# Two residual 5x5 convolution layers on one core: layer 1's v inside x's buffer, layer 2's row combinations by ScalarE and adding transfers, column filtering in more chunks of layer 2

## The chip, the cores and the metric

The kernel runs on one core of one Trainium2 chip. The metric is the device time of one execution in microseconds (us), median of the runs. A time taken from the profile belongs to one profiled execution.

## The reference

The input x is 8 images of 32 channels of 252 x 252 float32. Two layers of the same form follow each other:

```python
# _gn: normalisation over 16 groups of 2 channels; conv: 5x5, reflected borders, 32 -> 32 channels
x = x + _L0_conv_ref(_gn(x), L0_conv_weight)
x = x + _L1_conv_ref(_gn(x), L1_conv_weight)
```

The convolution's centre lies one pixel off (the reference shifts its weight by `-k // 2`, which is -3), so layer 1's result is kept with its own border columns and rows before layer 2 reads it.

## The kernel before, in words

**Layout.** An image is split by the parity of its columns and rows. The four parities of the 32 channels fill the 128 partitions, so the 5x5 filter becomes a 3x3 filter over 128 channels. The rows of an image are worked in 8 chunks of 16 rows of partitions (`ROWS`), in 4 groups of 4 (`NT`). In the code l is 0 for layer 1 and 1 for layer 2, b the image and c the chunk.

**Rows: a transform with six points.** Along the rows each group of four outputs is computed by six products at points 0 to 5 in place of twelve. `transform` makes the inputs of these points from the rows of a chunk (VectorE): v, differences of rows two apart (`row_pairs`), and u, two combinations "row + four times (or minus four times) another row" (`row_quads` L576 and L577, `last_rows` L584). From u come points 2 and 1 (`point2` L592, `point1` L602), from v points 4, 3, 0 and 5 (`point4` L596, `point3` L599, `points05` L609). For layer 2 v isn't made by VectorE: `row_sums` copies rows by a transfer that GpSimd issues (L557) and adds the others by two adding transfers (L559, L560). The copy waits until L609 of the chunk before has read the one buffer of v, the adding transfers wait for the copy.

**Columns: all or filtered.** `conv` multiplies on TensorE: three products for each of points 2, 4 (`m`, in PSUM), 1, 3 (`pairs`) and then 0, 5 (`sums`). In chunks for which `by_columns` says so, points 0 and 5 are column-filtered: `columns` (L612 on) makes sums and differences of neighbouring columns on VectorE, eight products of half width (L707) take the place of six of full width, and `column_parts` (L787 on) puts the halves together. ScalarE and VectorE move results out of PSUM (`seed`, `evacuate`, `difference`, `inner`, `outer`, `outer_columns`).

**Layer 1's result.** `keep` writes sums for layer 2's normalisation and the border columns of y (`reflect`: four narrow copies on ScalarE, L869 to L872). Layer 2's result is interleaved into o by ScalarE (L925) and stored.

**Loading x.** `load` (SP's queue) brings a chunk of x into one of two buffers xs; each row has 256 elements. For most chunks only the partitions of one column parity are loaded (`once`): they hold the odd columns, `even_columns` (ScalarE, L159) copies one into the other half of the partitions. GpSimd fills `borders` (L148 to L154). Layer 1's `transform` reads the even columns only.

**Order.** There is no scheduler: each step is entered in a table with a time in us, and the steps are issued in order of these times; at run time each engine follows its order and waits for semaphores.

```python
order = [(0, 0, c) for c in range(NCH)]
for k in range((B - 1) * NCH):
    order += [(1 + k // NCH, 0, k % NCH), (k // NCH, 1, k % NCH)]
```

So layer 1's chunk of one image alternates with layer 2's chunk of the image before. I call two such chunks a pair. `begin(i)` is the time at which slot i (the i-th chunk of `order`) starts on TensorE: 13.6 us from one slot to the next where both chunks are filtered. A chunk's transform runs in the slot before its own, its outputs of points 0 and 5 leave PSUM up to two slots later. For layer 2 `two` is the start of the slot two before its own, in which L557 (at `two` + 1.45) and L559 and L560 (at `two` + 8.4) stand.

Names that the steps touch: `row_sums`, `row_quads`, `last_rows`, `row_pairs`, `points05` and `columns` in `transform`; `column_parts` in `conv`; `reflect` in `keep`; `load`, `borders`, `even_columns`; `by_columns`. The pool `vpool` has one buffer for each tag; layer 1's v has the tag "v", layer 2's "va" (the last chunks use both), u has "u12".

Of the kernel before, what the change touches and what calls it, by code (L numbers as in the profile page):

```python
# [42 lines left out]
F32 = mybir.dt.float32  # L43
# [6 lines left out]
P = 128  # L50
# [6 lines left out]
def tile_conv_preact_x2(ctx: ExitStack, tc: tile.TileContext, x: bass.AP, w0: bass.AP, w1: bass.AP, out: bass.AP):  # L57
# [34 lines left out]
    def at(t: float, fn, *args, **kw):  # L92
        table.append((t, len(table), fn, args, kw))
# [67 lines left out]
    def once(b: int, c: int) -> bool:  # L161

        return c != NCH - 1 and (c != 1 if b > 1 else c != 3 if b else True)

    def copied_late(b: int, c: int) -> bool:

        return once(b, c) and (b > 1 or (b == 1 and c > 3))

    def parts(b: int, c: int):

        if once(b, c):
            return ((0, 10), (10, 6)) if (b, c) == (0, 0) else ((0, 2), (2, 14))
        return ((0, ROWS),) + (((ROWS, 2),) if c == NCH - 1 else ())
# [363 lines left out]
    def transform(t0: float, t1: float, b: int, l: int, c: int, free: float = -100.0, now=(0, 0, 0)):  # L537

        wi = WIN[l]
        got = {}  # L540
        sent = l == 1 and (b, c) != (0, 0)

        def source():
            if l == 0:
                nxt = xs[b, c + 1] if c + 1 < NCH else xtail[b]
                return xs[b, c][:, :, 0:256:2], nxt[:, :, 0:256:2]
            return ytile[b, c], ytile[b, c + 1] if c + 1 < NCH else ytail[b]

        def row_sums(add: bool):

            t, nxt = source()
            if not add:

                i = max(order.index((b, l, c)) - order.index((B - 2, 1, NCH - 2)), 0)
                got["v"] = vpool.tile([P, ROWS, wi], F32, tag=("va", "v")[i % 2], name=f"v_{b}_{l}_{c}")
                got["vt"] = got["v"].rearrange("p (t i) w -> p t i w", i=4)
                G.dma_start(got["v"], t)  # L557
            else:
                G.dma_start(got["v"][:, 0 : ROWS - 2], t[:, 2:ROWS], accum_op=ALU.add)  # L559
                G.dma_start(got["v"][:, ROWS - 2 : ROWS], nxt[:, 0:2], accum_op=ALU.add)  # L560

        def row_pairs(j0: int = 0, j1: int = NT):
            if j0 == 0:
                got["v"] = vpool.tile([P, ROWS, wi], F32, tag="v", name=f"v_{b}_{l}_{c}")
            v, (t, nxt) = got["v"], source()
            r0, r1 = 4 * j0, min(4 * j1, ROWS - 2)
            (V.tensor_add if l else V.tensor_sub)(v[:, r0:r1], t[:, r0 + 2 : r1 + 2], t[:, r0:r1])  # L567
            got["vt"] = v.rearrange("p (t i) w -> p t i w", i=4)

        def row_quads(j0: int = 0, j1: int = NT):  # L570
            if j0 == 0:
                got["u"] = vpool.tile([P, 2, NT, wi], F32, tag="u12", name=f"u12_{b}_{l}_{c}")
            u1, u2, (t, nxt) = got["u"][:, 0], got["u"][:, 1], source()
            r0, k1 = 4 * j0, min(j1, NT - 1)
            f = 4.0 if l else -4.0
            stt(u1[:, j0:j1], t[:, r0 + 1 : 4 * j1 : 4], f, t[:, r0 + 3 : 4 * j1 : 4], ALU.mult, ALU.add)  # L576
            stt(u2[:, j0:k1], t[:, r0 + 2 : 4 * k1 : 4], f, t[:, r0 + 4 : 4 * k1 + 1 : 4], ALU.mult, ALU.add)  # L577

        def last_rows():

            u2, (t, nxt) = got["u"][:, 1], source()
            if not sent:
                (V.tensor_add if l else V.tensor_sub)(got["v"][:, ROWS - 2 : ROWS], nxt[:, 0:2], t[:, ROWS - 2 : ROWS])
            stt(u2[:, NT - 1], t[:, ROWS - 2], 4.0 if l else -4.0, nxt[:, 0], ALU.mult, ALU.add)  # L584

        def point2(j0: int = 0, j1: int = NT):
            if j0 == 0:
                t = tpool.tile([P, 2, NT, wi], F32, tag="t24", bufs=1, name=f"t24_{b}_{l}_{c}")
                if not fixed:
                    fixed.append(vpool.tile([P, 2, NT, WMAX], F32, tag="t13", name="t13"))  # L590
                ts[b, l, c] = {0: t, 1: fixed[0][:, :, :, 0:wi]}
            V.tensor_sub(ts[b, l, c][0][:, 0, j0:j1], got["u"][:, 1, j0:j1], got["u"][:, 0, j0:j1])  # L592

        def point4(j0: int = 0, j1: int = NT):
            vt = got["vt"][:, j0:j1]
            stt(ts[b, l, c][0][:, 1, j0:j1], vt[:, :, 1], -2.0, vt[:, :, 2], ALU.mult, ALU.add)  # L596

        def point3():
            stt(ts[b, l, c][1][:, 1], got["vt"][:, :, 1], 2.0, got["vt"][:, :, 2], ALU.mult, ALU.add)  # L599

        def point1():
            stt(ts[b, l, c][1][:, 0], got["u"][:, 1], norm[b, l][1][:, 1:2], got["u"][:, 0], ALU.add, ALU.add)  # L602

        def points05():
            if by_columns(b, l, c):
                t = vpool.tile([P, NT, 2, wi], F32, tag="u12", name=f"t05_{b}_{l}_{c}")
            else:
                t = tpool.tile([P, NT, 2, wi], F32, tag="t05", name=f"t05_{b}_{l}_{c}")
            stt(t, got["vt"][:, :, 0:2], 4.0 if l else -4.0, got["vt"][:, :, 2:4], ALU.mult, ALU.add)  # L609
            ts[b, l, c][2] = t  # L610

        def columns():  # L612

            t, (m, mo) = ts[b, l, c][2], evens_odds(l)
            sd = vpool.tile([P, 2, NT, 2, m], F32, tag="sdiff", name=f"sdiff_{b}_{l}_{c}")
            d = tpool.tile([P, NT, 2, 2, m], F32, tag="t05", name=f"d05_{b}_{l}_{c}")
            odd, even = t[:, :, :, 1 : 2 * m : 2], t[:, :, :, 2 : 2 * m + 1 : 2]
            V.tensor_add(sd[:, 0], odd, even)
            V.tensor_sub(sd[:, 1], even, odd)
            if m == mo:  # L620
                f = "p t e (m a) -> p (t e) a m"
                V.tensor_sub(
                    d.rearrange("p t e a m -> p (t e) a m"),
                    t[:, :, :, 0 : 2 * m].rearrange(f, a=2), t[:, :, :, 2 : 2 * m + 2].rearrange(f, a=2),
                )
            else:
                V.tensor_sub(d[:, :, :, 0], t[:, :, :, 0 : 2 * m : 2], t[:, :, :, 2 : 2 * m + 1 : 2])
                V.tensor_sub(d[:, :, :, 1, 0:mo], odd[:, :, :, 0:mo], t[:, :, :, 3 : 2 * mo + 2 : 2])
            ts[b, l, c][2] = d, sd

        if (b, l, c) == order[0]:
            at(t0 - 33.3, row_quads, 0, 2)
            at(t0 - 31, point2, 0, 2)
            for fn in (row_pairs, point4):
                at(t0, fn, 0, 2)
            at(t0 + 0.2, row_quads, 2, 4)
            at(t0 + 0.2, row_pairs, 2, 4)
            at(t0 + 0.2, last_rows)
            at(t0 + 0.2, point2, 2, 4)
            at(t0 + 0.2, point4, 2, 4)  # L640
            at(t0 + 4.9, point1)
            at(t0 + 5.5, point3)
            at(t0 + 6.2, points05)
        else:
            if sent:
                two = begin(order.index((b, l, c)) - 2)
                at(two + 1.45, row_sums, False)
                at(two + 8.4, row_sums, True)
            else:
                at(t0, row_pairs)  # L650
            for dt, fn in ((2, row_quads), (3.2, last_rows), (3.6, point2)):
                at(t0 + dt, fn)
            at(max(t0 + 4.2, free + 9.45) if sent else t0 + 4.2, point4)
            at(max(t0 + 5.5, free + 7.8), point1)
            at(max(t0 + 5.6, free + (11.1 if by_columns(*now) else 10.25)), point3)
            at(t1, points05)
            if by_columns(b, l, c):
                at(t1 + 1.5, columns)
# [184 lines left out]
    def keep(t1: float, t2, b: int, c: int, got):  # L843
# [17 lines left out]

        def reflect():
            lo, hi = (1 if c == 0 else 0), (ROWS - 1 if c == NCH - 1 else ROWS)
            y, copy, r = got["y"], A.copy, slice(lo, hi)

            def negated(dst, src):
                A.activation(dst, src, AF.Copy, scale=-1.0)
# [101 lines left out]
    def by_columns(b: int, l: int, c: int) -> bool:  # L969
        if l == 0:  # L970
            return c < NCH - 1 and (b > 1 or (b == 1 and c > 1))
        return c in {B - 1: (1, 2, 3, 4, 5), B - 2: (1, 2, 3)}.get(b, (1, 2, 3, 5, 7))

    own = [5.1 if i in at_once else 1.7 if by_columns(*n) else 0.0 for i, n in enumerate(order)]
    late = [0.0 if i in at_once else 1.7 if by_columns(*n) else 5.1 for i, n in enumerate(order)]
# [60 lines left out]
    for i, (b, l, c) in enumerate(order):  # L1036
# [11 lines left out]
        if i + 1 < len(order):  # L1048
# [3 lines left out]
            if nl == 0 and 2 < k < len(inputs):  # L1052
                kb, kc = inputs[k]
                for part in parts(kb, kc):
                    if copied_late(kb, kc):
                        at(t0 + 9.5, load, kb, kc, *part)
                        at(begin(i + 2) + 4.0 if part[0] else t1 + 5.5, borders, kb, kc, *part)
                        at(begin(i + 3) + 4.0 if part[0] else t1 + 9.35, even_columns, kb, kc, *part)
                        continue
# [77 lines left out]
```

## Time and profile before

| | |
|---|---|
| Time, median of 3 runs (lowest, highest) | 1879.63 us (1878.62, 1879.75) |
| Profiled execution: its own time | 1879.27 us |
| Its span, first to last instruction | 1877.5 us |
| Mean granted TensorE clock | 0.994 |
| q1, transfers issued by SP: MB, share of the DMA engines' span | 230.73, 49.8% |
| q0, transfers issued by GpSimd: MB, share | 134.20, 29.3% |

Read a row of groups as: line, engine, operation, output<-input by the program's names, shape, count, then busy us and mean ns of one. A row of the timeline begins with start and duration in us. A row of windows gives for a stretch the busy us (and instructions) of PE, PEld, DVE, ACT and POOL, then the granted clock, the mean DMA share and GB/s. PE is TensorE, DVE VectorE, ACT ScalarE, POOL GpSimd. A row of waits says which engine and line waited for which: total us, times, longest.

### The profile page before, as it was taken

How to read it: one execution, taken by the hardware profiler on the slowest of the kernel's cores; microseconds unless marked ns; L12 is line 12 of the kernel's file. 1: busy time of each engine (PE TensorE's matmuls, PEld its weight loads, DVE VectorE, ACT ScalarE, POOL GpSimd, SP SyncE). 2: the span in 40 equal slices, each digit the busy share in tenths (PEclk: the TensorE clock that was granted, in tenths of full speed). 3: DMA queues.
4: the chain of work that ended last, by engine and by line, in shares of the span. 5: the costliest groups of instructions: out<-in, count | busy, mean ns of one | idle time of the engine just before them, and what ended most of it. 6: DMA issues, size and time to landing. Idle time of an engine off the chain costs nothing.

```text
span 1877.5 us, 20381 instructions
## 1 busy us (share of the span) xinstructions
PE 1839.2 (98%) x5194; PEld 966.0 (51%) x5194; DVE 1731.2 (92%) x3030; ACT 1493.8 (80%) x2781; POOL 396.2 (21%) x855
## 2 busy tenths in 40 slices
PE   5999999999999999999999999999999999999998
PEld 4444455545555555555555455554555555555455
DVE  7988799999999999999999899999999999997796
ACT  5886788878887888888898798987898876765575
POOL 4543111131112211122111311113111141110211
PEclk8999999999999999999999999999999999999999
DMA  9877578878888877987878967888878866775785
GB/s 275 203 179 180 151 209 199 210 194 202 217 202 219 194 209 192 221 223 173 220 193 206 235 175 205 205 204 204 212 202 198 214 165 140 179 174 148 195 212 125
DMA packets 207110, 369.07 MB, mean 197 GB/s; under 512 B 19088, under 2 KB 173968, under 8 KB 196752
## 3 DMA queue, kind: packets, MB, share of 16 engines
q1 hardware_dynamic: 178832, 230.73, 49.8%
q0 software_dynamic: 27600, 134.20, 29.3%
q10 hardware_dynamic: 560, 2.83, 0.4%
q8 instruction: 41, 0.67, 0.2%
q14 instruction: 77, 0.63, 0.1%
HBM read 167.15 MB, written 67.39 MB: 125 GB/s over the span
## 4 chain that ended last, share of the span: by engine, by line
PE 80%; DVE 7%; DMA 6%; ACT 3%; issue 3%; SPq 0%; POOL 0%; DVEq 0%; ACTq 0%; POOLq 0%
PE m L685 28%; PE pairs L685 28%; PE sums L707 7%; PE extra L707 6%; PE sums L685 6%; PE extra L685 4%; DMA v<-y 2%; DMA st<-in_x_dram 1%; DMA v<-ytail 1%; DMA xs<-in_x_dram 1%; ACT o L925 1%; DVE sd L748 1%; DVE t L609 1%; DMA wraw<-in_L_conv_weight_dram 1%; DMA out_dram<-o 0%
## 5 line engine op out<-in xcount | busy, mean ns | idle before, releaser
L685 PE MATMUL pairs<-t,u 128*128 128x504 f32 (+2 forms) x1548 | 692.9, 586 | 5.4 <-ACT pairs L729 3.3
L685 PE MATMUL m<-t,u 128*128 128x508 f32 (+3 forms) x1560 | 674.8, 581 | 3.4 <-DVE u L526 1.9
L685 PEld LDWEIGHTS m<-t,u 128*128 128x128 f32 x1560 | 294.2, 189 | 317.1 <-issue 297.0
L685 PEld LDWEIGHTS pairs<-t,u 128*128 128x128 f32 x1548 | 290.2, 189 | 320.1 <-issue 289.1
L925 ACT COPY o<-y 64x508 f32<-64x508 f32 x496 | 327.5, 660 | 8.6
L748 DVE SCALAR_TENSOR_TENSOR sd<-sd,pairs 128x504 f32<-128x504 f32 (+2 forms) x258 | 164.2, 671 | 19.5 <-PE pairs L685 15.2
L707 PEld LDWEIGHTS extra<-sdiff,wc 128*128 128x128 f32 x680 | 125.9, 189 | 98.1 <-issue 47.8
L707 PE MATMUL extra<-sdiff,wc 128*128 128x252 f32 (+3 forms) x680 | 173.0, 376 | 3.4 <-ACT extra L711 2.3
L860 ACT ACTIVATE junk<-y,negk 128x1008 bf16<-128x1008 f32 (+1 forms) x144 | 147.4, 1024 | 31.1 <-PE extra L707 14.5
L557 POOL DMA_DIRECT2D v<-y x63 | 35.7, 567 | 622.7 <-DVE t L609 608.4
L737 ACT COPY sd<-m 128x504 f32<-128x504 f32 (+2 forms) x258 | 136.9, 581 | 33.3 <-DVE sums L794 28.1
L609 DVE SCALAR_TENSOR_TENSOR t<-v 128x1024 f32<-128x1024 f32 (+1 forms) x128 | 157.7, 1232 | 5.4 <-PE sums L685 5.4
L707 PE MATMUL sums<-d,u 128*128 128x252 f32 (+3 forms) x680 | 157.4, 374 | 0.0
L707 PEld LDWEIGHTS sums<-d,u 128*128 128x128 f32 x680 | 127.6, 189 | 24.9 <-issue 9.0
L685 PE MATMUL sums<-t,u 128*128 128x508 f32 (+5 forms) x312 | 133.6, 577 | 0.0
L567 DVE TENSOR_TENSOR v<-xs 128x1792 f32<-128x1792 f32 (+1 forms) x65 | 130.2, 2003 | 1.2
L241 ACT ACTIVATE st<-st,negk 128x1134 f32<-128x1134 f32 x98 | 121.7, 1242 | 3.2
L559 POOL DMA_DIRECT2D v<-y x63 | 54.3, 862 | 329.1 <-DMA v<-y 329.1
L159 ACT COPY xs<-xs 64x1792 f32<-64x1792 f32 (+2 forms) x97 | 109.3, 1129 | 13.4 <-POOL xs L151 11.1
L729 ACT ACTIVATE pairs<-m,means 128x504 f32<-128x504 f32 (+1 forms) x129 | 84.2, 653 | 44.5 <-PE m L685 36.0
L785 ACT ACTIVATE y<-sums 128x504 f32<-128x504 f32 (+1 forms) x158 | 94.5, 634 | 28.3 <-PE sums L707 19.2
L235 ACT ACTIVATE st<-st 128x1134 f32<-128x1134 f32 x98 | 112.5, 1148 | 5.0 <-DMA st<-in_x_dram 3.2
(174 smaller groups left out, 2529.7 us busy)
## 6 DMA issues: line engine op xcount, KB each, us to landing
v<-y POOLq DMA_DIRECT2D x63, 1032.0 KB, 6.1
st<-in_x_dram SPq DMA_DIRECT2D x111, 567.0 KB, 6.1
out_dram<-o SPq DMA_DIRECT2D x480, 126.0 KB, 5.9
v<-y POOLq DMA_DIRECT2D x63, 903.0 KB, 7.7
xs<-in_x_dram SPq DMA_DIRECT2D x96, 441.0 KB, 8.4
xs<-in_x_dram SPq DMA_DIRECT2D x44, 504.0 KB, 12.0
u<-ud SPq DMA_DIRECT2D x15, 1152.0 KB, 6.0
xs<-in_x_dram SPq DMA_DIRECT2D x16, 472.5 KB, 9.3
```

The source lines that it names most:

```text
L159: copy(t[64:128, :, 0:256:2], t[0:64, :, 1:256:2])
L235: A.activation(junk, src, AF.Identity, accum_out=acc[:, 0, i : i + 1])
L241: A.activation(junk, src, AF.Square, bias=negk, accum_out=acc[:, 1, i : i + 1])
L567: (V.tensor_add if l else V.tensor_sub)(v[:, r0:r1], t[:, r0 + 2 : r1 + 2], t[:, r0:r1])
L609: stt(t, got["vt"][:, :, 0:2], 4.0 if l else -4.0, got["vt"][:, :, 2:4], ALU.mult, ALU.add)
L685: T.matmul(dst, u[:, k, 2 - i, :], rhs[:, j0 + i0 : j0 + i1, i : i + wo], start=(i == 0 and not add), stop=(i == 2), skip_group_check=add,)
L707: T.matmul(dst[:, 0, use], w, rhs[:, use], start=(i == 2), stop=True, skip_group_check=(i != 2))
L737: A.copy(got["sd"][:, 1 + e], m24[e][:, 0:n])
L748: stt(d, d, -2.0, pairs13[e][:, 0:n], ALU.mult, ALU.add)
L785: A.activation(y, src, AF.Copy, scale=1.0 - 2 * i, **total(3 * i))
L860: A.activation(dst, src, AF.Square, bias=negk, scale=1.0 if i else -1.0, accum_out=acc[:, 1, at_ : at_ + 1])
L925: copy(got["o", h][halves[s], 0:m, cp::2], got["y"][halves[cp], r : r + m, :])
```

## The change

1. Layer 1's v (from image 1, chunk 4 on) is written by VectorE into the odd columns of x's own buffer, which nothing reads after `even_columns`; it needs no buffer of its own. x's buffer is then released only after `points05`. So the loads two chunks later (`deferred`) are entered later, in two parts for all chunks.
2. For 50 chunks of layer 2 u isn't made by VectorE. ScalarE writes four times the rows into a buffer with the freed tag "v" (`four_times`), and GpSimd issues three adding transfers that add the other rows (`outer_rows`), ahead of the copy that begins v.
3. `by_columns` covers chunks 1 to 7 of layer 2 (before: 1, 2, 3, 5, 7), and 1 to 4 of the last image but one (before: 1 to 3).
4. The four copies of border columns in `reflect` are issued on GpSimd in chunks 1 to 6.

```diff
+    def among_columns(b: int, c: int) -> bool:
+        return b > 1 or (b == 1 and c > 3)
+    def deferred(b: int, c: int) -> bool:
+        i = inputs.index((b, c))
+        return i > 1 and among_columns(*inputs[i - 2])
     def parts(b: int, c: int):
+        if deferred(b, c):
+            return ((0, 2), (2, 14)) + (((ROWS, 2),) if c == NCH - 1 else ())
...
+        sent_u = l == 1 and (b, c) > (0, 4) and order[order.index((b, l, c)) - 1][1] == 0
...
+        def four_times():
+            got["u"] = vpool.tile([P, 2, NT, wi], F32, tag="v", name=f"ua_{b}_{l}_{c}")
+            src = source()[0].rearrange("p (t i) w -> p i t w", i=4)
+            A.activation(got["u"], src[:, 1:3], AF.Copy, scale=4.0)
+        def outer_rows():
+            t, nxt = source()
+            u1, u2 = got["u"][:, 0], got["u"][:, 1]
+            G.dma_start(u1, t[:, 3:ROWS:4], accum_op=ALU.add)
+            G.dma_start(u2[:, 0 : NT - 1], t[:, 4:ROWS:4], accum_op=ALU.add)
+            G.dma_start(u2[:, NT - 1], nxt[:, 0], accum_op=ALU.add)
         def row_pairs(j0: int = 0, j1: int = NT):
-            if j0 == 0:
+            if l == 0 and among_columns(b, c):
+                got["v"] = xs[b, c][:, :, 1:256:2]
+            elif j0 == 0:
                 got["v"] = vpool.tile([P, ROWS, wi], F32, tag="v", name=f"v_{b}_{l}_{c}")
...
                 at(two + 8.4, row_sums, True)
+                if sent_u:
+                    at(begin(order.index((b, l, c)) - 3) + 13.0, four_times)
+                    at(two + 1.4, outer_rows)
...
-            for dt, fn in ((2, row_quads), (3.2, last_rows), (3.6, point2)):
-                at(t0 + dt, fn)
+            for dt, fn in ((2, row_quads), (3.2, last_rows)):
+                if not sent_u:
+                    at(t0 + dt, fn)
+            at(t0 + 3.6, point2)
...
-            y, copy, r = got["y"], A.copy, slice(lo, hi)
+            y, copy, r = got["y"], A.copy if c in (0, NCH - 1) else G.tensor_copy, slice(lo, hi)
...
-        return c in {B - 1: (1, 2, 3, 4, 5), B - 2: (1, 2, 3)}.get(b, (1, 2, 3, 5, 7))
+        return c in {B - 1: (1, 2, 3, 4, 5), B - 2: (1, 2, 3, 4)}.get(b, (1, 2, 3, 4, 5, 6, 7))
...
+                    if deferred(kb, kc):
+                        at(t1 + 6.0, load, kb, kc, *part)
+                        at(begin(i + 2) + 10.0 if part[0] else t1 + 11.0, borders, kb, kc, *part)
+                        if once(kb, kc):
+                            at(begin(i + 3) + 4.0 if part[0] else t1 + 12.6, even_columns, kb, kc, *part)
+                        continue
```

## The prediction, before the result was known

> **What bounds the kernel now.** I read the busy shares, then the chain of waits, then the timeline of TensorE.
>
> ```profile
> PE 1839.2 (98%) x5194; PEld 966.0 (51%) x5194; DVE 1731.2 (92%) x3030; ACT 1493.8 (80%) x2781; POOL 396.2 (21%) x855
> ...
> PE 80%; DVE 7%; DMA 6%; ACT 3%; issue 3%; SPq 0%; POOL 0%; DVEq 0%; ACTq 0%; POOLq 0%
> ```
>
> TensorE is busy 98% of the span and carries 80% of the chain. A modelled busy time can hide small stalls, so I compare slots: a slot starts with a chunk's first `m` product.
>
> ```profile
> 717.64 5.27 PE L685 MATMUL m<-t,u 128*128 128x508 f32 x12
> 731.31 5.23 PE L685 MATMUL m<-t,u 128*128 128x504 f32 x12
> 744.86 5.27 PE L685 MATMUL m<-t,u 128*128 128x508 f32 x12
> 756.80 5.23 PE L685 MATMUL m<-t,u 128*128 128x504 f32 x12
> 773.76 1.44 PE L685 MATMUL m<-t,u 128*128 128x508 f32 x3
> ```
>
> 508 columns is layer 2, 504 layer 1. A pair (one chunk of each) with both chunks column-filtered takes 744.86 - 717.64 = 27.22 us. With layer 2's chunk 4 unfiltered it takes 773.76 - 744.86 = 28.90. The table's 27.2 and 28.9 are matched: TensorE loses nothing here. But VectorE is nearly as full:
>
> ```profile
> 719.88 1.23 DVE L609 SCALAR_TENSOR_TENSOR t<-v 128x1032 f32<-128x1032 f32 x1
> ...
> 740.58 0.70 DVE L576 SCALAR_TENSOR_TENSOR u<-y 128x516 f32<-128x516 f32 x1
> 741.19 0.56 DVE L577 SCALAR_TENSOR_TENSOR u<-y 128x387 f32<-128x387 f32 x1
> 741.66 0.29 DVE L584 SCALAR_TENSOR_TENSOR u<-y,y 128x129 f32<-128x129 f32 x1
> 742.05 0.70 DVE L592 TENSOR_TENSOR t<-u 128x516 f32<-128x516 f32 x1
> ...
> 748.12 1.23 DVE L609 SCALAR_TENSOR_TENSOR t<-v 128x1032 f32<-128x1032 f32 x1
> ```
>
> From one L609 of layer 2 to the next it runs without a gap for 28.24 us, more than TensorE's 27.22. It falls 1 us behind per filtered pair and recovers in the unfiltered ones (chunks 4 and 6). The DMA engines, in stretches of the filtered pair 676.9 to 704.1:
>
> ```profile
> 676.90:690.45 13.55, 13.55 (x42) 7.55 (x41) 13.38 (x23) 11.39 (x23) 1.31 (x3) 1.00 0.68 159
> 690.45:704.10 13.65, 13.65 (x42) 7.56 (x41) 13.51 (x22) 13.26 (x23) 2.82 (x6) 1.00 0.88 284
> ...
> 676.90:683.70 6.80, 6.80 (x18) 3.06 (x17) 6.76 (x10) 6.05 (x11) 1.31 (x3) 1.00 1.14 231
> 685.40:690.50 5.10, 5.10 (x22) 3.77 (x21) 5.00 (x12) 4.63 (x11) 0.00 (x0) 1.00 0.00 0
> ```
>
> The next-to-last column is the DMA share. It reaches 1.14 when loads and sums collide ([...] 1.00 is no ceiling), and there are 5.1 us with nothing moving. Layer 2's v is made by transfers that GpSimd issues:
>
> ```profile
> 721.41 0.55 POOL L557 DMA_DIRECT2D v<-y  x1 [13.03 <-DVE t L609]
> ...
> 727.16 0.87 POOL L559 DMA_DIRECT2D v<-y  x1 [4.68 <-DMA v<-y]
> 727.70 1.23 POOL L560 DMA_DIRECT2D v<-y  x1
> ...
> DMA to landing us min/median/max: 6.6/8.6/14.3
> ```
>
> The copy waits until L609 has released v, the sums wait for the copy, and the last sum (its landing is the bottom line) is needed by L596 at 743.34. 743.34 - 727.70 - 8.6 leaves 7.0 us. Over the steady batches, issue to L596 is 11.4 to 16.5 us, shortest in the pair of chunk 5: 2.8 us left there.
>
> [...] with GpSimd copying at 721.96 to 722.48, L793 to L794 took 0.71 us, and 0.71 also at 736.84 without any. [...]
>
> **The change, part by part.**
>
> *Column filtering.* The instruction order has 13 more layer-2 chunks filtered (chunks 4 and 6 of batches 0 to 5, chunk 4 of batch 6). Filtering puts eight products of 252 or 256 columns in the place of six of 508, so each saves TensorE 28.90 - 27.22 = 1.68 us: 13 x 1.68 = **-21.8 us**, all on the path while the others keep up. VectorE gains seven operations per converted chunk (four in `columns`, three in `column_parts`): 2.4 + 1.9 us by starts, 4.3. ScalarE gains one seed, 0.58.
>
> *Row combinations off VectorE.* In 50 layer-2 chunks L576, L577 and L584 go: 742.05 - 740.58 = 1.47 us. A filtered pair then needs 28.24 - 1.47 = 26.77 of VectorE against 27.22. It fits with 0.45 to spare, but now in six successive pairs; the pairs of chunks 7 and 0 keep one unfiltered chunk each and give it 28.90 - (26.77 - 4.3), about 6 us each, to catch up. So nothing for VectorE if nothing makes it wait. The change does add a wait: L592 needs ua's three transfers, and all of VectorE is queued behind it. By the order it comes about 20 us after they are issued, so they hide behind the pair's own work.
>
> *ScalarE.* `four_times` is one activation over 1032 elements: between 0.93 us (768, L515) and 1.15 (1134, L235), 1.09. It stands at the end of layer 1's slot, behind the small even-columns copy and before the eviction that opens the next slot. Four edge copies of 0.22 us leave for GpSimd in chunks 1 to 6. Net +0.2 in a slot that uses 11.4 of 13.55: cost 0, unless that copy waits for a late load.
>
> *v in x's odd columns.* No instruction more. Writing every second column costs nothing: L793 does, 675 ns against 672 for L763; reading likewise (L576 from xs 0.69, from y 0.70). But x's buffer is held until L609. Its load moves on SP's queue past four stores and a piece load into layer 1's slot, where the idle 5.1 us are. The release is about 2 us into that slot, and such loads take 5.8 (two rows) to 8.4 us to land. The two-row part is asked for at 11.0 by GpSimd's borders and at 12.6 by ScalarE's copy, so 2 to 4 us are left; VectorE needs it only near 19, the rest a slot later. Cost 0. If that cover is gone, GpSimd's adding transfers and v's copy, and ScalarE's `four_times` and eviction L785, are late next, since they stand right behind. 13 loads are now split, 52 more issues on SP and 39 more border copies on GpSimd; both wait rather than work.
>
> *Edge copies on GpSimd*, 48 x 4 of about 0.2 us: GpSimd works 21% of the span. They stand between layer 2's sums and the next chunk's borders, waiting for ScalarE's eviction; 0[...].
>
> *The three adding transfers* are unlike anything in the trace: 1024 rows of 516 B per chunk. By the trace's packet records an adding row takes 0.104 us at 1032 B and 0.558 at 7224 B, which is 0.028 + 0.073 per 1000 B, so 0.066 at 516 B: 1024 x 0.066 / 16 = 4.2 us of all engines (2.4 without the fixed part, 6.7 at 0.104). The idle 5.1 us hold it, barely. [...] at 0.55 us per 128 rows 4.4 us (1.6 if the count doesn't matter, 9.6 at L560's 1.2). [...] They can start 0.5 us into layer 2's slot, so the copy goes at 4.9 instead of 1.9 to 3.8, and its packets up to 1 us later still: v is late by 2 to 4, say 3.5 us. The ordinary pair's 7.0 us take that; chunk 5's 2.8 don't: 0.7 us in each of five batches, **+3.5 us**.
>
> *Sum*: against its own time, 1877.5 of span and 1.8 around it, 1879.3 - 21.8 + 3.5 = **1861.0**. The median of the runs, 1879.63, is 0.3 above; no correction.
>
> **Rivals.**
> - *v comes late in every pair* (slower). The point is 7.0 + 0.45 = 7.4 us of delay in an ordinary pair, 3.2 in chunk 5's. [...] the copy goes at 10.1, 8 us late: 0.6 us in 32 pairs and 4.8 in six, +48: about 1906. For it: POOL's longest waits are already in this chain (L557 on L609 608 us, L559 on its copy 329). Against it: today's waits of L596 for v are 25 us in total and TensorE lost none of it. 0.19.
> - *The DMA engines fill up* (slower). At 0.104 us per row the need is 6.7 us against 5.1 idle: 1.6 x 50 = 80, about 1938. The mixed stretches at 1.14 speak for it; that loads move into idle time, against. 0.05. Smaller mishaps [...] that just turn the sign: 0.03.
> - *Half the gain is eaten* by waits of VectorE, 8 to 18 us: 1866 to 1876. 0.10.
> - *No change*, filtering given back: 0.08. That the filtering isn't done is excluded by the instruction order.
>
> **How the numbers follow.** The forecast, 1857 to 1866, has 0.55; with the half-eaten case, faster has 0.65. About 0.2%, 3.8 us, is what a measurement can tell from none. Same 0.08, slower 0.19 + 0.05 + 0.03 = 0.27. Low end 1854: no allowance, and the roughly 0.7 us that TensorE loses per batch at the change of batch regained. High end 1897: it takes in the milder part of the first rival and leaves out about 0.14 above and 0.05 below.
>
> **What would show it.** Right: filtered pairs of 27.2 us in chunks 1 to 6, DVE about 26.8 of them, L596's waits for v near 30 us in total. Wrong: the first of the three adding issues over 2.5 us on POOL, L596 (or the new user of ua, L592) waiting for DMA by several us per pair, a DMA share near 1.1 throughout a pair, or slots over 13.7 us.

## The result and the profile after

The changed kernel takes 1979.41 us (median of 4 runs, 1974.59 to 1984.83) against 1879.69 for the kernel before on the same chip (1878.62 to 1884.56): ratio 1.0534, 95% interval 1.0512 to 1.0556. It is 99.7 us slower, where I had forecast 18.6 us faster. The profiled execution took 1976.06 us with a span of 1974.3.

New line numbers for what the prediction named: v's copy and sums (L557, L559, L560) are L570, L572, L573; L592 is L620, L596 is L624, L602 is L630, L609 is L637; the first write of y, L757, is L790; TensorE's products L685 and L707 are L718 and L740. New are `four_times` (L579) and the three adding transfers of `outer_rows` (L584 to L586). The kernels of the experiments that add lines above these have them 3 or 5 higher.

The page's busy shares and its chain of waits, of the kernel after:

```profile
PE 1845.1 (93%) x5246; PEld 979.0 (50%) x5246; DVE 1715.3 (87%) x2971; ACT 1517.0 (77%) x2652; POOL 656.0 (33%) x1236
...
PE 48%; DMA 15%; ACT 14%; DVE 11%; issue 8%; POOL 3%; SPq 1%; ACTq 0%; DVEq 0%; POOLq 0%
```

TensorE's share falls to 93%, and no engine has taken its place as the bound: VectorE is less busy than before, too. In the chain TensorE falls from 80% to 48%, and transfers, ScalarE, VectorE and "issue" grow. TensorE, VectorE and ScalarE all have a smaller share of a longer run, so I look for waits between them. The timeline of TensorE says where:

```profile
806.51 5.27 PE L718 MATMUL m<-t,u 128*128 128x508 f32 x12
820.18 5.23 PE L718 MATMUL m<-t,u 128*128 128x504 f32 x12
833.74 5.27 PE L718 MATMUL m<-t,u 128*128 128x508 f32 x12
848.67 5.23 PE L718 MATMUL m<-t,u 128*128 128x504 f32 x12
870.00 5.27 PE L718 MATMUL m<-t,u 128*128 128x508 f32 x12
894.60 7.18 PE L718 MATMUL m<-t,u 128*128 128x504 f32 x12 [11.27 <-issue]
```

The pair 806.51 to 833.74 takes 27.23 us, as forecast. But the slot from 870.00 to 894.60, layer 2's chunk 7 of batch 2, takes 24.6 us where the table of slots has 11.9. Over six batches that slot has a mean of 23.82 us; it was 12.80 before. VectorE in that slot (columns: start, duration, line, tiles; in brackets the idle time ahead and what ended it):

```profile
881.62 1.27 DVE L781 SCALAR_TENSOR_TENSOR sd<-sd,pairs 128x508 f32<-128x508 f32 x2
892.54 0.69 DVE L790 SCALAR_TENSOR_TENSOR y<-pairs,sd 128x508 f32<-128x508 f32 x1 [9.65 <-DMA v<-y]
893.15 0.68 DVE L791 SCALAR_TENSOR_TENSOR y<-sd 128x508 f32<-128x508 f32 x1
893.74 0.69 DVE L627 SCALAR_TENSOR_TENSOR t<-xs 128x512 f32<-128x512 f32 x1
894.35 0.15 DVE L384 TENSOR_SCALAR var<-m 128x1 f32<-128x1 f32 x1
```

L790 doesn't read v. It *writes* y, and waits 9.65 us for a transfer "v<-y". The transfers in question, on GpSimd:

```profile
871.19 1.31 POOL L584 DMA_DIRECT2D ua<-y  x1
872.00 1.79 POOL L585 DMA_DIRECT2D ua<-y  x1
872.75 1.96 POOL L586 DMA_DIRECT2D ua<-y  x1
873.36 1.92 POOL L570 DMA_DIRECT2D v<-y  x1
885.69 0.85 POOL L572 DMA_DIRECT2D v<-y  x1 [10.41 <-DMA v<-y]
```

They make u and v of chunk 0 of batch 3, from y_3_0_0 (y of batch 3, layer 1, chunk 0). The nine buffers of `ypool` are handed out again as their tiles are read for the last time. In the kernel before VectorE still reads y_3_0_0 (L576, L577) twelve instructions after its first write of y of (2, 1, 7), so that this y got another buffer. With those reads moved to transfers, the last readers of y_3_0_0 are transfers issued in this very slot: in the order of the program the pool gives y_2_1_7 this buffer, and L790 must wait until L572, issued at 885.69, has read it. In the instruction order VectorE's first write of y waits for transfers of GpSimd in eight places, and in none before: in chunk 7 of layer 2 of batches 0 to 5, in y_6_1_1 and in y_7_0_6.

Behind L790 stands L384, which reads batch 3's variance out of a column of `m`, in PSUM. TensorE's next `m` products write the same tile. L384 starts at 894.35 and takes 0.15 us; they start at 894.60, after 11.27 us idle. They are also slow, 7.18 us in the place of 5.27: the granted clock from 894.60 to 901.80 is 0.74. After the six waits of this kind the twelve products take 13.2 us more in all than in the kernel before. ScalarE's root L386 waits for the same L384, and the scaling of layer 2's weights for that. The kernel's waits show this chain (columns: total us, times, longest):

```profile
ACT std L386 <- DVE var L384: 74.1, 10, 12.3
PE m L718 <- issue: 63.0, 6, 11.3
DVE y L790 <- DMA v<-y: 35.7, 5, 9.7
DVE t L624 <- DMA v<-y: 26.0, 12, 4.3
DVE y L790 <- issue: 24.5, 3, 9.0
DVE t L624 <- issue: 17.0, 7, 4.2
```

L790 waited 60 us in eight cases, TensorE's `m` 63 us in six. "issue" at L790 is the same wait, where the profile has no event for its end. That it accounts for all of the loss is not shown by this list; the first experiment takes this wait away.

### The profile page after: what moved, and what is told of

Read it like the earlier page. It is cut to its first block, busy times and chain, and to the rows that moved or that the text cites. A ratio compares the mean times of both kernels' runs of the same rounds, so it can differ in the third digit from the quotient of the medians.

```text
span 1974.3 us, 21016 instructions
## 1 busy us (share of the span) xinstructions
PE 1845.1 (93%) x5246; PEld 979.0 (50%) x5246; DVE 1715.3 (87%) x2971; ACT 1517.0 (77%) x2652; POOL 656.0 (33%) x1236
## 4 chain that ended last, share of the span: by engine, by line
PE 48%; DMA 15%; ACT 14%; DVE 11%; issue 8%; POOL 3%; SPq 1%; ACTq 0%; DVEq 0%; POOLq 0%
PE pairs L718 17%; PE m L718 17%; DMA v<-y 11%; PE extra L740 4%; PE sums L740 3%; ACT o L958 3%; PE extra L718 3%; PE sums L718 3%; ACT junk L893 2%; DMA out_dram<-o 2%; ACT st L246 2%; ACT ua L579 1%; DMA st<-in_x_dram 1%; DVE sd L781 1%; ACT y L818 1%
## 5 line engine op out<-in xcount | busy, mean ns | idle before, releaser
L718 PE MATMUL m<-t,u 128*128 128x508 f32 (+3 forms) x1560 | 686.6, 590 | 66.1 <-issue 63.0
L718 PE MATMUL pairs<-t,u 128*128 128x504 f32 (+2 forms) x1548 | 700.2, 589 | 14.8 <-ACT pairs L762 7.0
L718 PEld LDWEIGHTS m<-t,u 128*128 128x128 f32 x1560 | 298.7, 192 | 387.0 <-issue 368.1
L718 PEld LDWEIGHTS pairs<-t,u 128*128 128x128 f32 x1548 | 290.3, 190 | 331.0 <-issue 291.0
L740 PE MATMUL extra<-sdiff,wc 128*128 128x256 f32 (+3 forms) x784 | 203.7, 381 | 16.2 <-ACT extra L744 10.7
L740 PEld LDWEIGHTS extra<-sdiff,wc 128*128 128x128 f32 x784 | 144.0, 189 | 131.3 <-issue 62.3
L572 POOL DMA_DIRECT2D v<-y x63 | 53.5, 849 | 442.9 <-DMA v<-y 426.6
L740 PE MATMUL sums<-d,u 128*128 128x252 f32 (+3 forms) x784 | 182.2, 375 | 0.0
L148 POOL COPY xs<-xs 64x4 f32<-64x4 f32 (+3 forms) x126 | 71.6, 568 | 311.4 <-DMA xs<-in_x_dram 271.4
L740 PEld LDWEIGHTS sums<-d,u 128*128 128x128 f32 x784 | 146.7, 189 | 21.9 <-issue 1.9
L790 DVE SCALAR_TENSOR_TENSOR y<-pairs,sd 128x504 f32<-128x504 f32 (+1 forms) x129 | 87.0, 674 | 60.2 <-DMA v<-y 35.7
L494 POOL TENSOR_TENSOR u<-u,resid 32x64 f32<-32x64 f32 x180 | 79.6, 442 | 164.5 <-ACT u L526 154.3
L570 POOL DMA_DIRECT2D v<-y x63 | 96.4, 1530 | 111.2 <-DVE t L637 86.0
L818 ACT ACTIVATE y<-sums 128x504 f32<-128x504 f32 (+1 forms) x184 | 109.3, 634 | 24.4 <-PE sums L740 16.6
L584 POOL DMA_DIRECT2D ua<-y x50 | 64.7, 1295 | 186.3 <-ACT ua L579 186.3
```

The source lines that it names most:

```text
L718: T.matmul(dst, u[:, k, 2 - i, :], rhs[:, j0 + i0 : j0 + i1, i : i + wo], start=(i == 0 and not add), stop=(i == 2), skip_group_check=add,)
L740: T.matmul(dst[:, 0, use], w, rhs[:, use], start=(i == 2), stop=True, skip_group_check=(i != 2))
L790: stt(yrow(2), s1, 4.0 * f, s0, ALU.mult, op, **total(2))
L818: A.activation(y, src, AF.Copy, scale=1.0 - 2 * i, **total(3 * i))
```

## The experiments

I compare kernels by the sum of what their slots lose against the table (the time from one chunk's first `m` product to the next one's, less the slot's planned length), with the times of three kinds of slots by themselves, six batches each: layer 2's chunk 7, layer 1's chunk 7, and layer 1's chunk 0 that follows. The losses are those of the profiled executions. Each ratio is against runs of the kernel before in the same session (medians 1878.45 to 1880.16 us). The table's sum is 1793.5 us with the filtering of before, 1771.4 with that of the change, and 1781.6 with chunk 6 left unfiltered.

| kernel | median us | ratio to before, 95% | lost in all | layer 2, chunk 7 | layer 1, chunk 7 | next chunk 0 |
|---|---|---|---|---|---|---|
| before | 1879.69 | 1 | 18.9 | 5.4 | 3.1 | 0.2 |
| after | 1979.41 | 1.0534 (1.0512 to 1.0556) | 140.8 | 71.5 | 15.5 | 10.4 |
| touch0 | 1914.69 | 1.0202 (1.0163 to 1.0240) | 80.0 | 17.8 | 13.7 | 2.2 |
| u_on_dve | 1920.08 | 1.0218 (1.0194 to 1.0241) | 84.5 | 17.8 | 33.8 | 4.0 |
| no_filter | 1943.10 | 1.0330 (1.0301 to 1.0360) | 85.6 | 4.6 | 6.6 | 36.2 |
| filter_only | 1918.68 | 1.0220 (1.0189 to 1.0250) | 80.7 | 18.8 | 31.9 | 0.8 |
| no6 | 1894.13 | 1.0082 (1.0065 to 1.0098) | 46.3 | 4.6 | 7.8 | -1.7 |
| ulate | 1989.18 | 1.0591 (1.0560 to 1.0621) | 154.8 | 17.8 | 34.3 | 4.3 |
| both | 1965.63 | 1.0478 (1.0442 to 1.0513) | 117.7 | 7.6 | 10.5 | 1.0 |
| add_only | 1892.55 | 1.0074 (1.0059 to 1.0090) | 31.5 | 4.6 | 7.3 | -1.7 |
| uearly | 1932.29 | 1.0290 (1.0273 to 1.0306) | 94.5 | 21.7 | 9.4 | 5.3 |
| no6_uearly | 1919.67 | 1.0224 (1.0210 to 1.0239) | 74.6 | 4.6 | 7.9 | 4.8 |
| no6_u45 | 1871.84 | 0.9967 (0.9955 to 0.9979) | 26.1 | 4.6 | 5.7 | -1.7 |
| parts14 | 1875.61 | 0.9969 (0.9956 to 0.9981) | 14.9 | 4.6 | 2.3 | -1.6 |

### touch0: y's buffer held longer, nothing else

```diff
+        def touch():
+            A.copy(tiny("held", b, c), source()[0][:, 0, 0:1])
...
                 at(two + 8.4, row_sums, True)
+                if c == 0 and sent_u:
+                    at(two + 12.0, touch)
```

> The changed kernel with one thing added: for chunk 0 of layer 2 (batches 1 to 7), ScalarE copies one column of y to a spare tile at two + 12.0, after VectorE's first write of y_b_1_7, so that y_b_1_7 gets another buffer than the one whose last readers are v's and u's transfers; some 0.2 us of ScalarE more in seven slots, nothing else. Theory A (the change frees y_b_1_0's buffer for y_(b-1)_1_7 early, whose first write on VectorE then waits for the transfers that were issued in the same slot): the slot of chunk 7 falls from about 23 us to about 13, and six times 10 to 12 us go: 1905 to 1918. Theory B (VectorE is late at chunk 7 anyway, after six filtered pairs, and the wait at y only shows it; or the adding transfers delay v): the wait moves to another line, the slot stays at 20 us or more, and the time is 1965 to 1980.

Measured: 1914.69 us, 64.7 less than the changed kernel, for seven copies of one column. Layer 2's chunk 7 takes 14.86 us on average, in the place of 23.82. VectorE at L790's place (L795 here), in batch 3:

```profile
1091.53 1.27 DVE L786 SCALAR_TENSOR_TENSOR sd<-sd,pairs 128x508 f32<-128x508 f32 x2
1092.71 0.68 DVE L795 SCALAR_TENSOR_TENSOR y<-pairs,sd 128x508 f32<-128x508 f32 x1
1093.31 0.68 DVE L796 SCALAR_TENSOR_TENSOR y<-sd 128x508 f32<-128x508 f32 x1
```

No bracket, no wait. Theory A holds for these 65 us, though the slot falls to 14.86 and not to about 13; B predicted that the wait would only move. But 35 us above the kernel before are left, 54 above my forecast.

### u_on_dve, no_filter, filter_only: one part of the change undone, or done alone

u_on_dve is the changed kernel with `sent_u = False` (u's rows on VectorE in all chunks):

> The changed kernel with u's row combinations on VectorE again in all chunks (no four times on ScalarE, no three adding transfers); filtering, v in x's odd columns and the edge copies on GpSimd stay. Theory A (the buffer): y of chunk 7 doesn't wait for transfers any more, so the 66 us of the six slots of chunk 7 go; VectorE has 1.47 us more work per pair than in the changed kernel, 28.2 in pairs of 27.2, which costs up to 1 us in six pairs of each batch, at most 40: 1915 to 1950. Theory B (VectorE late at chunk 7): VectorE being later still, the slot of chunk 7 loses as much as now or more: 1980 to 2010.

no_filter is the changed kernel with

```diff
-        return c in {B - 1: (1, 2, 3, 4, 5), B - 2: (1, 2, 3, 4)}.get(b, (1, 2, 3, 4, 5, 6, 7))
+        return c in {B - 1: (1, 2, 3, 4, 5), B - 2: (1, 2, 3)}.get(b, (1, 2, 3, 5, 7))
```

> The changed kernel with layer 2's chunks filtered as before (chunks 1, 2, 3, 5 and 7); everything else of the change stays, and y_b_1_7 still has the buffer that v's and u's transfers read. Theory A (the buffer): the slots of chunk 7 still lose some 10 us each for six batches, about 60, and the 21.8 us of filtering are not gained: 1935 to 1960. Theory B (VectorE late after six filtered pairs): chunks 4 and 6 give VectorE its time back, the slot of chunk 7 loses next to nothing: 1875 to 1890.

filter_only is the kernel before with this line changed the other way:

> The kernel before with only the filtering of chunks 4 and 6 added (row combinations and edge copies as before). Theory A (the buffer is the loss, filtering is not): VectorE needs 28.2 us in pairs of 27.2 and can't keep up in six pairs on end: most of the 21.8 us are eaten, 1862 to 1895, and no slot loses 10 us. Theory B (filtering makes VectorE late at chunk 7): the slot of chunk 7 loses 10 us or more in each of six batches: 1920 to 1960.

u_on_dve came to 1920.08 and no_filter to 1943.10, both within what theory A gave and far from B. In no_filter the wait is there without any crowding of VectorE; it comes out a slot later, as 36.2 us in layer 1's chunk 0.

filter_only, 1918.68, misses A's range and all but reaches B's: 39.6 us *slower* than before, from an edit that takes 22.1 us off the table. No transfer is added there, no write of y waits for one, and still chunk 7 loses 31.9 us in layer 1 and 18.8 in layer 2 over six batches. So B was wrong for the wait at y, and right that filtering makes chunk 7 lose. TensorE at the start of that slot, batch 4; first the kernel before, then filter_only:

```profile
1038.10 5.23 PE L685 MATMUL m<-t,u 128*128 128x504 f32 x12
1043.32 0.35 PE L346 MATMUL m<-mv,avg_ss 128*128 128x1 f32 x2
1043.76 2.78 PE L685 MATMUL pairs<-t,u 128*128 128x504 f32 x6
```

```profile
1062.12 5.23 PE L685 MATMUL m<-t,u 128*128 128x504 f32 x12
1070.28 0.35 PE L346 MATMUL m<-mv,avg_ss 128*128 128x1 f32 x2 [2.93 <-DVE mv L336]
1070.71 4.48 PE L685 MATMUL pairs<-t,u 128*128 128x504 f32 x6
```

L346 averages the statistics of the next batch over the groups. It stands in TensorE's own queue, right behind the slot's first products, and needs `mv`, a few tiny operations of VectorE. VectorE comes to them 4.9 us into the slot in the kernel before, and at 7.8 after six filtered pairs. Of these 2.9 us 1.25 are lateness (its first write of y in this slot starts at 1.60 us in the place of 0.35); most of the rest are chunk 6's own three operations of `column_parts` (L792 to L794, 1.9 us), which now stand just ahead. So VectorE's work turns into a stall of TensorE where TensorE needs a *result in time* rather than a rate. In the slots before it the lateness costs only some 0.3 to 0.8 us each. In touch0, where u's operations are off VectorE, the same wait is 1.1 to 2.2 us.

The stall costs more than its length. The six products that follow take 4.48 us, in the kernel before 2.78; the granted clock is 0.58 from 1070.28 to 1074.00, and 1.00 at this place in the kernel before. Over the six batches TensorE waits 17.5 us for `mv`, and these products take 11.0 us more: nearly all of the 28.8 us that layer 1's chunk 7 loses more than before.

### no6 and ulate: the two suspects for the rest

no6 is touch0 with chunk 6 of layer 2 left unfiltered:

```diff
-        return c in {B - 1: (1, 2, 3, 4, 5), B - 2: (1, 2, 3, 4)}.get(b, (1, 2, 3, 4, 5, 6, 7))
+        return c in {B - 1: (1, 2, 3, 4, 5), B - 2: (1, 2, 3, 4)}.get(b, (1, 2, 3, 4, 5, 7))
```

> touch0 with chunk 6 of layer 2 unfiltered, as in the kernel before (chunks 1 to 5 and 7 filtered); by the table that gives back 6 x 1.68 = 10.1 us. Theory C (what is left of the loss is VectorE, which after six filtered pairs comes late to the statistics of chunk 7, so that TensorE waits there for the mean): the slots of layer 1's and layer 2's chunk 7 return to the 0.4 and 0.8 us lost of before, 4 to 6 us less per batch, 25 to 35 in six: 1888 to 1900. Theory D (what is left comes from the adding transfers, which make v late): the 10.1 us are simply lost: about 1925.

Measured: 1894.13. By undoing filtering worth 10.1 us, 20.6 us are won: 33.7 us less are lost, and layer 2's chunk 7 is back at 4.6. So filtering chunk 6 costs them, and theory C's range holds. Its mechanism holds only in part: in layer 2's chunk 7 of touch0 VectorE isn't late. Its first write of y starts 12.8 us into that slot, against 12.7 to 14.5 in the kernel before. What has moved is the variance. The kernel before (y of batch 2, L373 reads batch 3's variance):

```profile
842.36 0.15 DVE L373 TENSOR_SCALAR var<-m 128x1 f32<-128x1 f32 x1
846.45 0.68 DVE L757 SCALAR_TENSOR_TENSOR y<-pairs,sd 128x508 f32<-128x508 f32 x1
```

In the changed kernel L384 stands *behind* L790 (above). The steps of layer 2's statistics are entered at a fixed time from the start of layer 1's chunk 7 (`te = t0 + 15.3`). The table makes that slot 20.4 us long with chunk 6 unfiltered and 17.0 with it filtered, so they fall 3.4 us later in layer 2's chunk 7. In every run with chunk 6 filtered the variance is read some 1.8 us after this write of y starts, in every run without it at least 4.0 us before (batches 0 to 5). TensorE's next `m` products wait for that read: 1.5 us in each of six slots of touch0, nothing in no6. This order is also why the wait at y stopped TensorE at once in the changed kernel, and a slot later in no_filter. No run moved the statistics' steps alone, so how much of the 33.7 us is this order and how much VectorE's load stays open.

ulate is touch0 with the adding transfers behind v's on GpSimd's queue:

```diff
-                    at(two + 1.4, outer_rows)
+                    at(two + 8.45, outer_rows)
```

> touch0 with u's three adding transfers issued after v's copy and sums (two + 8.45 in the place of two + 1.4); all six pairs filtered. Theory D (issued ahead of v's copy, they make v late by their own time): L627's waits for transfers fall from 30.7 us to under 10, the slots of layer 2's chunks 3, 4 and 6 and of layer 1's chunk 4 lose what they lost before, about 4 us less per batch: 1888 to 1900. Theory C (VectorE is late at chunk 7): slots of chunks 3 and 4 may gain, those of chunk 7 stay: 1905 to 1915; and if u comes too late now (12 us are left until VectorE reads it), the wait moves to L623 and the time is 1915 to 1940.

Measured: 1989.18, 74.5 slower than touch0 and beyond every range that I gave. VectorE's waits tell where (ulate):

```profile
DVE t L623 <- DMA ua<-y: 123.1, 40, 10.1
```

L623 is the reader of u. VectorE's waits for v, 46.8 us in touch0, are gone from the list, and 123.1 us have come for u, since v's sums and u's rows now move at the same time, just ahead of their readers. Of the 20 us that I had counted between u's issue and its use, seven were moved away, and the other 12 weren't enough. The place `two` + 1.4 was the better of these two.

### both and add_only

both combines the three edits: chunk 6 unfiltered, u's transfers at `two` + 8.45, and `touch` in all chunks with u by transfers.

> Three edits to the changed kernel: one column of y is read by ScalarE at two + 12.0 in every chunk whose u comes by transfers (not only chunk 0), so that no y gets a buffer that such transfers read; u's adding transfers go after v's; chunk 6 of layer 2 is unfiltered. If theories C and D are both right and add up: 1914.7 - 4.6 (the slot of layer 1's chunk 2 in batch 7) + 10.1 - 30 - 24 = 1866, 1862 to 1878, below the kernel before. If one of them is wrong: 1885 to 1900.

Measured: 1965.63, beyond both ranges. ulate's loss is in it. It is 23.6 less than ulate, near no6's 20.6, but `touch` in the other chunks differs as well.

add_only is no_filter with `touch` in all chunks that have u by transfers. It asks what u's transfers cost by themselves, with the filtering of before and no wait at y:

> The changed kernel with the filtering of before (chunks 1, 2, 3, 5 and 7) and with one column of y read by ScalarE at two + 12.0 in every chunk whose u comes by transfers, so that no y waits for them; u's transfers stay ahead of v's. Theory C (VectorE's lateness costs, the adding transfers don't): as before, 1876 to 1882. Theory D (the adding transfers make v late): some 3 us lost per batch in the slots of chunks 2 to 4: 1890 to 1900. If the 34 us that the unfiltered kernel with the transfers lost at layer 1's chunk 0 are not the buffer's, they stay: about 1925.

Measured: 1892.55, as theory D had it. 50.5 us less than no_filter, so the 36.2 us at layer 1's chunk 0 were the buffer's as well. What is left over before is v that comes late (add_only):

```profile
DVE t L627 <- issue: 42.1, 11, 5.6
DVE t L627 <- DMA v<-y: 17.4, 9, 3.5
```

59.5 us of waiting for v, where the kernel before has 24.8 (17.6 for y's rows, 7.2 for the last chunk's). TensorE loses part of it, above all in layer 2's chunks 2 and 3, layer 1's chunk 4 and layer 1's chunk 7.

### uearly and no6_uearly: u's transfers out of v's way

uearly is the changed kernel with `touch` in all chunks that have u by transfers, and

```diff
-                    at(begin(order.index((b, l, c)) - 3) + 13.0, four_times)
-                    at(two + 1.4, outer_rows)
+                    at(begin(order.index((b, l, c)) - 3) + 9.0, four_times)
+                    at(begin(order.index((b, l, c)) - 3) + 9.5, outer_rows)
```

> The changed kernel, all six pairs filtered, one column of y read by ScalarE at two + 12.0 in every chunk whose u comes by transfers (no y gets a buffer that they read), and u made a slot earlier: four_times at 9.0 and the three adding transfers at 9.5 of the slot before the one in which v is copied, so that they are over when v's copy begins. Theory D (the adding transfers cost by standing ahead of v's copy): L627's waits for transfers, 30.7 us in touch0, fall under 10 and the slots of layer 2's chunks 2 to 4 and 6 lose nothing: with the 4.6 us of the slot in batch 7 gone as well, 1885 to 1900. Rival (in that slot they collide with x's loads, which then come late to GpSimd's borders and ScalarE's even columns): the waits move there, 1905 to 1930.

no6_uearly adds the unfiltered chunk 6:

> As uearly, with chunk 6 of layer 2 unfiltered. If theories C (VectorE late at chunk 7) and D (u's transfers ahead of v's copy) hold and add up: no6's 1894.1 less 5 (the slot in batch 7) less some 12 for v: 1873 to 1881, at best 5 us below the kernel before. If u's early transfers collide with x's loads: 1890 to 1910.

Measured: 1932.29 and 1919.67, 17.6 slower than touch0 and 25.5 slower than no6. VectorE's waits for v fell from touch0's 46.8 us to 1.3, as D had it. But it is not x's loads that pay, as my rival had it; GpSimd's wait for them fell from 269.8 us (touch0) to 60.0. In the stretch that I followed it is ScalarE's queue (uearly, ScalarE in layer 1's slot, then one of GpSimd's border copies):

```profile
964.97 1.07 ACT L579 ACTIVATE ua<-y 128x1032 f32<-128x1032 f32 x1 [1.10 <-DVE t L633]
965.94 0.57 ACT L749 ACTIVATE extra<-extra 128x504 f32<-128x504 f32 x1
...
971.62 0.42 ACT L159 COPY xs<-xs 64x256 f32<-64x256 f32 x1 [1.46 <-POOL xs L151]
972.05 1.15 ACT L823 ACTIVATE y<-sums 128x512 f32<-128x512 f32 x2
...
969.23 2.36 POOL L151 COPY xs<-xs 64x2 f32<-64x2 f32 x1
```

`four_times` now waits for L633, the last reader of the previous u (u has a single buffer), and the even-columns copy waits for GpSimd's borders. These stand behind the adding transfers, from 968.46 on, and last until 971.6. Each of the three copies takes 1.9 to 2.4 us; in touch0, at 728.04 to 728.94, they take 0.18, 0.18 and 0.65. In uearly VectorE works meanwhile on L630, L801, L802 and L640, of which only L801 reads PSUM (see the edge copies below). The two waits of ScalarE together are 2.6 us of a slot that ScalarE had nearly filled, and the eviction L823 and the next seed come late for it: VectorE waits 1.79 us for L823 at 973.23, and TensorE 0.78 us for ScalarE's seed. TensorE's waits for that seed (L767) grow from 9.4 us in touch0 to 18.1. That this is the whole loss is not shown.

### no6_u45: relief only where it is short

```diff
-        sent_u = l == 1 and (b, c) > (0, 4) and order[order.index((b, l, c)) - 1][1] == 0
+        sent_u = l == 1 and (b, c) > (0, 4) and c in (4, 5) and order[order.index((b, l, c)) - 1][1] == 0
...
-        return c in {B - 1: (1, 2, 3, 4, 5), B - 2: (1, 2, 3, 4)}.get(b, (1, 2, 3, 4, 5, 6, 7))
+        return c in {B - 1: (1, 2, 3, 4, 5), B - 2: (1, 2, 3, 4)}.get(b, (1, 2, 3, 4, 5, 7))
```

> The changed kernel with chunk 6 of layer 2 unfiltered and u by four_times and adding transfers in chunks 4 and 5 only (the other chunks' row combinations on VectorE), so that VectorE is relieved in the last two of five filtered pairs; y's buffers then aren't read by such transfers ahead of a write. If the loss of the change is the sum of what was found (y's buffer, VectorE late at chunk 7, the adding transfers in chunks 2 to 4 and 7), almost all of it is gone, and seven chunks more are filtered than before, 11.8 us by the table: 1868 to 1876, faster than the kernel before. If VectorE, 1 us short in each of chunks 1 to 3, can't make it up in 4 and 5: 1878 to 1890.

Measured: 1871.84, ratio 0.9967 (0.9955 to 0.9979): faster than both kernels, by 6.8 us against the kernel before in the same session. The page's busy shares (no6_u45):

```profile
PE 1828.3 (98%) x5222; PEld 967.5 (52%) x5222; DVE 1741.7 (93%) x3040; ACT 1480.1 (79%) x2609; POOL 554.1 (30%) x1125
```

TensorE is at 98% again, with 10.9 us less work than before.

### parts14: what the two small parts do alone

parts14 is no_filter with `sent_u = False`: only v in x's odd columns and the edge copies on GpSimd are left.

> The changed kernel with the filtering of before (chunks 1, 2, 3, 5 and 7) and u's row combinations on VectorE in all chunks: only layer 1's v in x's odd columns, with its later and split loads, and the edge copies on GpSimd are left of the change. Theory D (the 14 us that add_only lost against the kernel before are the adding transfers'): the time of before, 1876 to 1882. Rival (they come from the later loads of x, or from the edge copies): 1886 to 1894.

Measured: 1875.61, ratio 0.9969 (0.9956 to 0.9981). These two parts cost nothing and even bring 4.5 us. VectorE's waits for v, 24.8 us in the kernel before, are gone from its list. So what add_only lost more, 16.9 us between the medians, comes with u by `four_times` and adding transfers (and add_only's `touch` copies, 0.2 us of ScalarE each). And it puts no6_u45 in its place: against parts14 its 11.9 us of table are met by 11.2 us more of lost slots. Both have the same ratio to before. What makes no6_u45 faster, as far as these runs can tell, is what parts14 has; the filtering of chunk 4 brought no gain that could be measured.

## Why the prediction was wrong

By the profiled executions, the loss splits along the kernels: after to touch0, 60.8 us less lost (y's buffer); touch0 to no6, 33.7 less (chunk 6 filtered, the statistics late); no6 to add_only, 14.8 less (chunk 4 filtered, with 6.7 of it in one slot of batch 7 where the wait at y was left in no6); add_only to parts14, 16.6 less (u by adding transfers); from parts14 to before 4.0 are added. Together 121.9, the difference of 140.8 and 18.9. The table gives back 22.1, and 99.8 us remain, as measured.

The steps, in the prediction's order:

- **13 x 1.68 = -21.8 on the table**: right. The instruction order has it, and undisturbed pairs take 27.23.
- **"So nothing for VectorE if nothing makes it wait"**: this is the step that failed, in two ways: two waits were put at nothing. I listed the reader that the change makes wait (L592 for u) and not the *writer*: taking VectorE's reads of y away changed the last reader of y_3_0_0, hence the buffer of y_2_1_7, hence a wait at L790, 60.8 us. The diff shows nothing of it; the instruction order with its waits, which I had used for counts only, does.
- **"the pairs of chunks 7 and 0 ... give it about 6 us each, to catch up"**: the rate was right (between two L637 of layer 2 the changed kernel's VectorE needs 29.51 us with a wait of 2.81 in it, 26.70 without; I had 26.77). The place was wrong: the statistics of chunk 7 are wanted *ahead* of the catching up, behind chunk 6's own new operations, and with the shorter slot the variance comes behind a write of y. Six chunk-6 conversions, booked as 10.1 us of gain, lose 33.7 in the slots, 20.6 net by the medians. The sum also had no term for slow products: a wait of TensorE was priced at its length.
- **Adding rows and their issue, +3.5**: mis-sized; u by transfers cost 16.6. A row took 0.0726 us on average (median 0.067), near my 0.066, and the three issues with the start of the copy are 0.8, 0.8 and 0.6 us apart, 2.2 in all, half of the 4.4 that I had estimated from L557's 0.55 us for 128 rows. So u's rows are still moving when v's copy is issued: in the packet records of after the last of them ends 5.6 us behind that issue, and the copy's first packet starts 4.6 us behind it, in the kernel before 1.4 (medians). I had allowed "up to 1 us" for that, from no measurement; the copy's median time to landing rose from 6.1 to 9.0 us, by the pages of before and after, and is 6.0 in parts14 and 5.9 in uearly, where u's rows go first. With the copy issued 1.3 us later in its slot than in parts14 (medians 4.1 and 2.8), v is some 4 us late, near my 3.5. It was the cover that I had wrong: I took the median landing, 8.6 us, for every pair. In the kernel before L596 already waits for v in chunk 5 of batches 0 to 6, by 0.9 to 3.5 us, where I had 2.8 us left; and add_only waits in chunks 1, 3 and 6 as well as 5, where I had 7.0. My claim that u's transfers "hide behind the pair's own work" held at `two` + 1.4 (no wait for u shows), and failed at 8.45.
- **Loads into the idle 5.1 us, v in x's odd columns, edge copies on GpSimd, 0 each**: right, better than 0 (parts14). But VectorE's 0.71 us with and without a copying GpSimd say nothing of operations with both inputs in SBUF: L793 and L794 read `extra`, which lies in PSUM. With such operations GpSimd's copies do take longer. In parts14 the edge copies that start while VectorE runs one take 0.67 us in the median (73 of 192), the others 0.21; in after it is 0.67 (76 of 192) and 0.21. The kernel doesn't pay for it.
- **ScalarE +0.2, cost 0**: not measured apart; in add_only it is part of the 16.6. uearly shows how little it takes.
- **What would show it wrong**: L624's waits, forecast near 30 us, are 43.0 with those marked "issue". The DMA share in the pair 806.51 to 833.74 (next-to-last column) was over 1 in both slots, which I had named as a sign against me:

```profile
806.51:820.18 13.67, 13.67 (x42) 7.56 (x40) 13.53 (x22) 13.42 (x24) 4.26 (x5) 1.00 1.17 265
820.18:833.74 13.56, 13.56 (x42) 7.55 (x41) 10.72 (x17) 9.14 (x18) 5.00 (x12) 1.00 1.07 229
```

TensorE lost nothing in this pair: the share alone doesn't tell. But at its end, at 832.46, L624 had waited 2.81 us for v, and the slot after it, 833.74 to 848.67, took 14.93 in the place of 13.6.

Of the rivals, "v comes late in every pair" was right in kind, at a third of its weight (16.6 us against 48). None held the two larger causes. Left open: how no6's 33.7 us divide between VectorE's load and the order of the statistics; why filtering chunk 4 loses so much of what it saves (between add_only and no6 8.1 us of 11.9, the slot of batch 7 left out; between parts14 and no6_u45 11.2 of 11.9, with u's transfers in chunks 4 and 5 in it); and which of parts14's two edits takes v's waits away. None of these was tried.

## What to carry to other kernels

When a read is moved from an engine to a transfer, ask who gets the buffer next: the transfer is now its last reader, and the next writer waits for it, on whatever engine and in whatever chunk the pool decides. Compare the waits of the instruction order before and after, not only its counts. Where an engine runs as full as another, look for the places where a small result is due at a fixed point; slack counts up to there, not over the round. And when a change alters the length of a slot, see which steps are entered at fixed times from its start: they change places with others in the order.

## What was unexpected of the hardware

Two DMA issues on GpSimd can overlap in the trace: L585 has a record of 1.79 us, but L586 starts 0.75 us after it. Adding up such records would have given 5.1 us for three issues that took 2.2.

A short transfer delayed a long one by more than its bytes suggest: u's rows are a fifth of v's and u's bytes together, and v's copy took half as long again to land (9.0 us in the place of 6.1, medians). Counted by rows it fits: 1024 rows at the measured 0.0726 us, over 16 engines, are 4.6 us (an estimate), of which some 2.4 are left when the copy starts 2.2 us after the first issue; it lands 2.9 us later than before.

After these waits TensorE was slow for some us. Twelve `m` products behind a wait of 8.5 to 11.3 us took 1.8 to 2.7 us more (after; granted clock 0.74 behind the one at 894.60), six behind 2.9 us 1.5 to 2.7 more (filter_only; 0.58 behind the one at 1070.28). So in these runs a stall of TensorE that recurs cost more than the sum of its waits.
